# A graph convolution that gathers node rows: two columns of x by one addition, fewer row buffers, sums in one place

## The chip, the cores and the metric

The kernel runs on one core of a Trainium2 chip. The metric is the device time of one execution in microseconds, the median of several runs. A profile of one further execution gives the times of single instructions.

## The reference

There are 12,500 nodes with 128 features each (32 scalars and 32 vectors of three) and 412,500 directed edges, sorted by their destination. For each edge the features of the source node, multiplied by a weight matrix, are combined with weights that a small network makes from the 8 radial inputs of the edge; the messages are summed for each destination, multiplied once more, added to x, and normalised over the features.

```python
f0 = x0 @ W1_0e / sqrt(MUL);  f1 = einsum('nui,uw->nwi', x1, W1_1o) / sqrt(MUL)
feat0, self0 = f0[:, :MUL], f0[:, MUL:];  feat1, self1 = f1[:, :MUL], f1[:, MUL:]
e0 = feat0[edge_src];  e1 = feat1[edge_src]            # one row per edge
h = gelu(gelu(edge_scalar_attr @ W_mlp1 / sqrt(8)) @ W_mlp2 / sqrt(64))
w00, w01, w10, w11 = h @ Wp_00, h @ Wp_01, h @ Wp_10, h @ Wp_11
out0_a = w00 * e0 * ea0;  out0_b = w11 * sum(e1 * ea1[:, None, :], -1) / sqrt(3)
out1_a = (w01 * e0)[:, :, None] * ea1[:, None, :];  out1_b = w10[:, :, None] * e1 * ea0[:, :, None]
n0, n1 = segment_sum(concat(out0_a, out0_b)), segment_sum(concat(out1_a, out1_b))   # by edge_dst
y = cos(MIX) * self + sin(MIX) * (n0 @ W2_0e, n1 @ W2_1o)
return layernorm(x + y)
```

## The kernel before, in words

**Tiling.** The edges are cut into 806 runs of 512 (`NS`), a run into four blocks of 128 (`Q`). Two runs make a pair (`PR`, 403 of them), four a chunk (`CH`, 202). The main loop goes over pairs. The order of the instructions of PE, ACT, DVE and SP is the order of the program, written out by hand; POOL only issues gathers, in their own order, and each waits for its buffer.

**Where a block's rows come from.** Each block of 128 edges needs 128 feature rows in a tile `G` (edge by feature). There are five ways:

- An indirect DMA of POOL gathers 128 rows by index from a table in DRAM (`gather`, L223). The table holds all nodes' features and is made by the preamble (`turn`, `features_of`, `store_nodes`).
- DVE copies single columns out of `xT`, the transposed x that lies in SBUF, at addresses that it loads into registers (`fetch`, L174; `copy_columns`, L188); 128 of these make a tile that PE multiplies by the weights (L197), and ACT writes the product into `G` (L198). This serves block 2 of some runs.
- ACT does the same for block 1 of other runs (L192).
- SP copies the rows of block 3 singly, 128 DMAs of one row, for every 14th run from run 36 (`aid`, L204 and L208).
- The first 18 runs (`RAW`) come before the table is there: POOL gathers rows of x itself, which PE turns and multiplies (`turn_rows`, `features`, L616).

`SLOTS` says how many columns DVE and ACT copy at each of their places in a chunk's two pairs: DVE 60 and 68, ACT 56 each. `FROM` is the pair at which this begins, 6. `LEAD` is the number of runs for which there are `G` buffers, 20, ten pairs in all.

**The rest of a pair.** DVE multiplies the weights `w` (in PSUM) and `G` to the messages `M` in three instructions (`messages`: L651, and twice L655), PE sums them by segments (`segments`, L671), DVE places them in the running sums `acc` (`add`, L711), and for each group of 512 nodes (`GN`) that is complete the sums are multiplied and normalised (`norm`, L756 to L777; two groups at a time, `LNB`). The small steps of the normalisation stand in a list `waiting` and are taken between DVE's copies. When the window of sums moves on by 512 nodes, ACT copies `acc` into a second buffer, and DVE clears the new part in the four next pairs (L425). Indices come for 128 runs at a time (`load_indices`, L468 to L485).

Of the kernel before, what the change touches and what calls it, by code (L numbers as in the profile page):

```python
# [21 lines left out]
P = 128  # L22
# [17 lines left out]
LEAD = 20  # L40
# [17 lines left out]
def gnn_kernel(ctx: ExitStack, tc: tile.TileContext, x, src, dst, ea4, ea8, w1_0, w1_1, wm1, wm2,  # L58
# [31 lines left out]
    x_at, _ = nc.bump_sbuf(4 * N)  # L90
    xT = nc.alloc_sbuf_tensor_at("xT", [P, N], F32, offset=x_at).ap()
    x_bytes = xT.bitcast(U8)
    x_bytes = bass.AP(tensor=x_bytes.tensor, offset=x_bytes.offset - x_at, ap=[[4 * N, P], [1, x_at + 4 * N]])
# [16 lines left out]
    G, GP, GT, Y = {}, {}, {}, {}  # L110
# [12 lines left out]
    assert AID_FROM >= raw_runs and AID_LEAD < LEAD and P % ROWS == 0 and STEPS <= AID  # L123
# [7 lines left out]
    def aid_load():  # L131


        nc.sync.dma_start(aid_at, sub(src, AID_FROM * SB + (Q - 1) * P, [[AID * SB, len(aided)], [1, P]]))
        for e, g in picked.items():
            n, w = len(g) * P, per_chunk[e]
            flat = dr.tile([n], I32, name=f"flat{list(picked).index(e)}")
            cycle = next(c for c in range(1, len(g) + 1)
                         if all(g[i + c] - g[i] == g[c] - g[0] for i in range(len(g) - c)))
            for i in range(min(cycle, len(g))):  # L140
                k = len(g[i::cycle])
                step = g[i + cycle] - g[i] if k > 1 else 1
                nc.sync.dma_start(sub(flat, i * P, [[cycle * P, k], [1, P]]),
                                  sub(src, g[i] * SB + COL_Q[e] * P, [[step * SB, k], [1, P]]))
            for r in range(0, -(-n // w), P):
                k = min(P, -(-n // w) - r)
                full, rest = divmod(min(n - r * w, k * w), w)
                rows = cst.tile([k, w], I32, name=f"pick{len(pick_tiles)}")
                if rest:
                    nc.vector.memset(rows, 0)  # L150
                    nc.sync.dma_start(rows[full:full + 1, :rest], sub(flat, (r + full) * w, [[rest, 1], [1, rest]]))
                if full:
                    nc.sync.dma_start(rows[:full], sub(flat, r * w, [[w, full], [1, w]]))
                pick_tiles.append(rows)
                pick_rows[e, r // P] = rows
# [3 lines left out]
    def addresses():  # L159
        nc.vector.tensor_scalar(aid_at, aid_at, float(4 * P), None, op0=OP.mult)  # L160
        for rows in pick_tiles:
            nc.vector.tensor_scalar(rows, rows, 4.0, float(x_at), op0=OP.mult, op1=OP.add)
# [3 lines left out]
    def fetch(e, n):  # L166

        at = taken[e]
        n = min(n, len(picked[e]) * P - at)
        if n <= 0:  # L170
            return []
        taken[e] += n
        row, c0 = divmod(at, per_chunk[e])
        _, r = nc.values_load_multi_w_load_instructions(  # L174
            pick_rows[e, row // P][row % P:row % P + 1, c0:c0 + n], engines=[e], min_val=x_at,
            max_val=x_at + 4 * (N - 1), skip_runtime_bounds_check_because="addresses of columns")
        return [(at + k, r[k]) for k in range(n)]

    def copy_columns(e, columns):

        for at, r in columns:
            i, j = divmod(at, P)
            if j == 0:
                GT[e, i] = wk.tile([P, P], F32, name=f"gt{list(picked).index(e)}", bufs=3)
            to = GT[e, i][:, j:j + 1]
            col = x_bytes[:, bass.ds(r.with_bounds(guaranteed_mod_val=0, out_of_modulus=4), 4)].bitcast(F32)
            if e == DVE:
                nc.vector.tensor_copy(to, col)  # L188
                if waiting and j % 2:
                    waiting.pop(0)()  # L190
            else:
                nc.scalar.activation(to, col, AF.Copy)  # L192
# [7 lines left out]
    def aid(s, t):  # L200

        i = aided.index(s)
# [4 lines left out]
        for k in range(r1 - r0):  # L207
            nc.sync.dma_start(G[s][r0 + k:r0 + k + 1, Q - 1, :].bitcast(U8),  # L208
                              table_bytes[bass.ds(r[k], P * 4)].rearrange("(a k) -> a k", a=1))

    def gather(s):
        b, c = divmod(s, P)
        if s % PR == 0:
            GP[s // PR] = wk.tile([P, PR, Q, P], F32, name="G", bufs=LEAD // PR)
        G[s] = GP[s // PR][:, s % PR]
# [12 lines left out]
    diag = cst.tile([P, P], I32)  # L228
    nc.gpsimd.iota(diag, pattern=[[1, P]], base=0, channel_multiplier=-1)
    iota = cst.tile([P, P], F32)  # L230
# [23 lines left out]
    def load_nodes(b, rows=x):  # L254
        n0, nn, full, tail, _ = group(b)
        xt = wk.tile([P, XB, P], F32, name="xt", bufs=3)
# [32 lines left out]
    def turn(b):  # L289
# [5 lines left out]
        nc.scalar.activation(xT[:, n0:n0 + nn], PX[b][:, :nn], AF.Copy)  # L295

    def features_of(b):
        n0, nn, full, tail, tiles = group(b)
        pf = W2.pop(b)[:, 1].rearrange("p (q e) -> p q e", q=XB)
        for t, k in tiles:  # L300
            nc.tensor.matmul(pf[:k, t, :], xT[:, n0 + t * P:n0 + t * P + k], wf, start=True, stop=True)
        PF[b] = wk.tile([P, XB, P], F32, name="ft", bufs=3)
# [15 lines left out]
    scratch = wk.tile([P, 4, ACC], F32, name="acc")  # L318
# [102 lines left out]
    def new_sums():  # L421
        A["next"] = wk.tile([P, 4, ACC], F32, name="acc")

    def clear_sums(k):
        nc.vector.memset(A["next"][:, k, ACC - GN:], 0.0)  # L425
# [26 lines left out]
    def rows_tile(part=None):  # L452

        if part is None:
            return wk.tile([P, XB, P], F32, name="xt", bufs=3).rearrange("p q e -> p (q e)")
# [5 lines left out]
    def load_indices(b):  # L461
        ns = min(P, NS - b * P)
        idx[b] = wk.tile([P, Q, P], I32, name="idx")
        rel[b] = wk.tile([P, Q, P], F32, name="rel")
        colv[b] = wk.tile([P, P], F32, name="colv")
        for kind, raw in zip((1, 0), raws.pop(b)):
            f = wk.tile([P, XB, P], F32, name="ft", bufs=3).rearrange("p q e -> p (q e)")
            nc.vector.tensor_copy(f[:ns, :], raw[:ns, :])  # L468
            if kind:
                g = wk.tile([P, XB, P], F32, name="ft", bufs=3).rearrange("p q e -> p (q e)")  # L470
# [53 lines left out]
    def load_attributes(b):  # L524
        full, rest = divmod(min(E - b * P * P, P * P), P)
        t = e4_raw[b] = rows_tile(None if b else 2)
# [7 lines left out]
    def turn_attributes(b):  # L534
# [4 lines left out]
        e4[b] = wk.tile([P, 4, P], F32, name="e4")  # L539
# [63 lines left out]
    def turn_rows(s):  # L603
# [4 lines left out]
        XR[s] = wk.tile([P, Q, P], F32, name="xt", bufs=3)  # L608
# [35 lines left out]
    def messages(p, part):  # L644
        n = min(PR, NS - p * PR)
        if part == 0:
            M[p] = wk.tile([P, PR, Q, 2, P], F32, name="M")
        w, g, m = (t[:, :n].rearrange(f"p r q {k} -> p (r q) {k}") for t, k in
                   ((WP[p], "u"), (GP[p], "u"), (M[p], "a u")))
        if part == 0:  # L650
            nc.vector.tensor_tensor(m[:, :, :, :MUL], w[:, :, :2 * MUL].rearrange("p q (a u) -> p q a u", a=2),  # L651
                                    g[:, :, None, :MUL].to_broadcast([P, n * Q, 2, MUL]), op=OP.mult)
            return
        j = part - 1
        nc.vector.tensor_tensor(m[:, :, j, MUL:].rearrange("p q (i u) -> p q i u", i=3),  # L655
                                w[:, :, None, (2 + j) * MUL:(3 + j) * MUL].to_broadcast([P, n * Q, 3, MUL]),
                                g[:, :, MUL:].rearrange("p q (i u) -> p q i u", i=3), op=OP.mult)

    def segments(p):
# [3 lines left out]
        if r == 0:  # L663
            SEG[c] = ps.tile([P, CH, P], F32, name="seg", bufs=1)
            SG[c] = wk.tile([P, CH, P], F32, name="sg")
# [13 lines left out]
    def placing(c):  # L679
# [3 lines left out]
        PL[c] = wk.tile([P, CH, P], F32, name="pl")  # L683
# [19 lines left out]
    def add(c):  # L703
# [6 lines left out]
        a = A["now"][:, :, bass.ds(FIRST.pop(c), SPAN)]  # L710
# [7 lines left out]
    def moments(b, sums=None, half=None):  # L718
# [14 lines left out]
        for t, k in tiles:  # L733
            nc.tensor.matmul(pt[:k, t - t0, :], xT[:, n0 + t * P:n0 + t * P + k], ws, start=True, stop=sums is not None)
            if sums is None:
                for a in range(4):
                    nc.tensor.matmul(pt[:k, t - t0, :], A["now"][:, a, at + t * P:at + t * P + k], wpost[:, a, :],
# [105 lines left out]
    def general():  # L843
        T = max(t for t in range(1, P + 1) if E % t == 0)
        sums = dr.tile([N + P, P], F32)
        zero = wk.tile([P, XB, P], F32, name="ft", bufs=3)
# [4 lines left out]
        below = cst.tile([P, P], F32)  # L851
        nc.vector.tensor_scalar(below, diag, 0.0, None, op0=OP.is_lt)
# [100 lines left out]
    with tc.manual_schedule(engines={PE, ACT, DVE, SP}):  # L953
# [4 lines left out]
        for s in range(min(LEAD - 2, raw_runs)):  # L958
# [4 lines left out]
        for b in range(min(3, NG)):  # L963
# [4 lines left out]
        new_sums()  # L968
# [3 lines left out]
                 NG // 2 + 1: lambda: nc.vector.memset(A["next"], 0.0),  # L972
                 NG - 3: run_places}
        for b in range(NG + 2):
# [6 lines left out]
            if b + 3 < NG:  # L981
                XT[b + 3] = load_nodes(b + 3)
# [5 lines left out]
        for c in range(1, min(EDGES_AHEAD, NCH)):  # L988
            load_edges(c)
# [4 lines left out]
        for c in range(1, min(3, NCH)):  # L994
            radial(c)
# [11 lines left out]
        A["now"] = A["next"]  # L1007
# [16 lines left out]
        for p in range(NP):  # L1024
            c, k = divmod(p, CH // PR)
            mine = [s for s in range(p * PR, (p + 1) * PR) if s < NS]
            if p:
                for s in mine:
                    if s + LEAD - PR < NS:
# [15 lines left out]
            if k == 0:  # L1045
                placing(c)
                if c + 1 < NCH:
                    hot_rows(c + 1)
# [18 lines left out]
            if k == 0 and c > 0:  # L1067
                place(c - 1)
                placed = c
            if nets:  # L1070
# [6 lines left out]
            for s in mine:  # L1077
                if s % ET == 20 and s - 20 + ET < NS:
# [17 lines left out]
            if moved:  # L1096
                new_sums()
                clearing += list(range(4))
            elif clearing:
                clear_sums(clearing.pop(0))  # L1100
# [5 lines left out]
            picks(DVE, p, 2)  # L1106
            if k == 1 and placed > added:
# [8 lines left out]
            if p == 0:  # L1116
                addresses()
                find_first()
                new_sums()
                clearing = list(range(4))  # L1120
# [10 lines left out]
        for c in range(added, NCH):  # L1131
            if c >= placed:
                place(c)
            if moving and moving[0] + 2 == c:
                move_sums()
                moving.pop(0)
            add(c)
# [37 lines left out]
```

## Time and profile before

| | |
|---|---|
| median of 3 runs | 3540.56 us (3540.39 to 3550.26) |
| the profiled execution's own time | 3552.97 us |
| its span, first to last instruction | 3551.2 us |
| busy: PE, DVE, ACT, POOL | 73%, 88%, 81%, 75% |
| table gathers of POOL (L223) | 2728, mean 945 ns |
| column copies of DVE (L188) | 25,216 |
| column copies of ACT (L192) | 21,888 |
| row DMAs of SP (L208) | 7040 |
| mean granted TensorE clock | 0.819 |

A row of the costliest groups gives line, engine, operation, the tiles out and in, the count, the busy time and the mean duration in ns, and the idle time of the engine just before them with what ended most of it. A row of the timeline gives the start and the duration in us, then the same names. "issue" is time in which the engine waited for nothing that the profile shows.

### The profile page before, as it was taken

What the parts mean: (1) busy time and instruction counts of PE and PEld (TensorE: products, weight loads), DVE (VectorE), ACT (ScalarE), POOL (GpSimd) and SP (SyncE); (2) the same over time, 40 slices, a digit from 0 to 9 for tenths busy, and PEclk for the clock granted to TensorE, in tenths of its full rate; (3) what the DMA queues carried; (4) which work ended last, traced back from release to release, by engine and by line L of the source; (5) the groups of instructions that cost most, each with busy time, mean ns of one, the idle gap of its engine ahead of it and who ended that gap; (6) DMA issues with size and microseconds to landing.
All of it is one profiled execution on the core that took longest, in us unless ns stands there. A gap on an engine that the chain in (4) does not pass through costs nothing.

```text
span 3551.2 us, 141354 instructions
## 1 busy us (share of the span) xinstructions
PE 2577.7 (73%) x30219; PEld 1955.6 (55%) x30219; DVE 3113.3 (88%) x27933; ACT 2884.6 (81%) x24128; POOL 2647.6 (75%) x2807
## 2 busy tenths in 40 slices
PE   6777677777777777777776677676777777677775
PEld 5555555555555555555555555555555555555554
DVE  3499999999999988998988998888898888899886
ACT  2489889888898887888888788888798797788883
POOL 7677777777777777777777777777777777777775
PEclk9888888888788877788777787878788877788778
DMA  8222222223222222222222222222222222222221
GB/s 199 65 57 72 64 60 70 63 61 75 63 64 66 63 61 69 68 61 63 68 60 69 69 61 63 65 64 68 64 63 63 61 69 63 62 68 63 61 65 46
DMA packets 576956, 239.39 MB, mean 67 GB/s; under 512 B 481293, under 2 KB 526456, under 8 KB 576088
## 3 DMA queue, kind: packets, MB, share of 16 engines
q0 software_dynamic: 89600, 183.68, 18.0%
q1 hardware_dynamic: 465718, 40.13, 9.1%
q10 hardware_dynamic: 20770, 6.47, 0.8%
q8 instruction: 244, 4.00, 0.4%
q14 instruction: 624, 5.11, 0.4%
HBM read 217.25 MB, written 12.99 MB: 65 GB/s over the span
## 4 chain that ended last, share of the span: by engine, by line
DVE 35%; POOL 15%; issue 11%; ACT 10%; PE 9%; DMA 6%; SPq 6%; DVEq 4%; ACTq 1%; POOLq 0%
DVE gt L188 19%; POOL G L223 15%; DVE M L655 7%; ACT gt L192 7%; DMA G<-table,idx 6%; SPq L208 4%; DVEq L174 4%; DVE M L651 3%; DVE S L640 2%; PE w L598 2%; SPq L204 1%; PE m L698 1%; DVE pl L684 1%; DVE acc L711 1%; ACT h L560 1%
## 5 line engine op out<-in xcount | busy, mean ns | idle before, releaser
L223 POOL DMA_INDIRECT G<-table,idx x2728 | 2578.4, 945 | 853.3 <-issue 734.3
L192 ACT ACTIVATE gt<-xT 128x1 f32 x21888 | 2192.7, 190 | 116.3 <-issue 94.7
L188 DVE COPY gt<-xT 128x1 f32 x25216 | 1674.6, 144 | 141.4 <-issue 118.3
L655 DVE TENSOR_TENSOR M<-w,G 128x768 f32<-128x768 f32 x806 | 760.7, 944 | 0.0
L671 PE MATMUL seg<-M,S 128*32 128x128 f32 x12896 | 573.0, 323 | 122.1 <-DVE M L655 120.2
L571 PE MATMUL h<-h,w2b 64*64 64x256 f32 x3232 | 399.1, 516 | 311.6 <-ACT eT L546 208.6
L671 PEld LDWEIGHTS seg<-M,S 128*32 128x32 f32 x12896 | 393.3, 128 | 312.9 <-DVE M L655 178.9
L598 PE MATMUL w<-wpb,h 64*128 64x128 f32 x6448 | 565.3, 325 | 0.0
L598 PEld LDWEIGHTS w<-wpb,h 64*128 64x128 f32 x6448 | 476.5, 223 | 61.4 <-issue 27.0
L651 DVE TENSOR_TENSOR M<-w,G 128x512 f32<-128x512 f32 x403 | 275.4, 683 | 171.2 <-DMA G<-table,idx 64.5
L571 PEld LDWEIGHTS h<-h,w2b 64*64 64x64 f32 x3232 | 175.0, 169 | 437.2 <-ACT eT L546 259.6
L560 ACT ACTIVATE h<-h 128x512 f32<-128x512 f32 x404 | 234.9, 582 | 206.7 <-PE h L555 194.1
L197 PE MATMUL h<-wf,gt 128*128 128x128 f32 x736 | 202.0, 378 | 258.3 <-DVE gt L188 136.0
L197 PEld LDWEIGHTS h<-wf,gt 128*128 128x128 f32 x736 | 134.4, 237 | 349.6 <-issue 124.6
L698 PE MATMUL m<-pl,sg 128*128 128x128 f32 x1612 | 282.6, 329 | 20.8 <-ACT sg L677 20.3
L698 PEld LDWEIGHTS m<-pl,sg 128*128 128x128 f32 x1612 | 278.5, 245 | 30.0 <-ACT sg L677 26.2
L555 PE MATMUL h<-eT,w1b 64*128 64x128 f32 x3232 | 279.3, 304 | 21.1 <-ACT eT L546 14.8
L577 ACT ACTIVATE h<-h 128x512 f32<-128x512 f32 x404 | 234.5, 582 | 56.6 <-PE h L571 54.8
L555 PEld LDWEIGHTS h<-eT,w1b 64*128 64x128 f32 x3232 | 233.3, 205 | 57.9 <-ACT eT L546 15.0
L677 ACT ACTIVATE sg<-seg 128x256 f32<-128x256 f32 x403 | 148.7, 369 | 140.4 <-PE seg L671 135.5
L640 DVE TENSOR_TENSOR S<-oh,m 128x512 f32<-128x512 f32 x202 | 134.7, 667 | 9.5 <-ACT m L633 8.5
L684 DVE TENSOR_TENSOR pl<-m,colv 128x512 f32<-128x512 bf16 x202 | 137.1, 679 | 0.0
(123 smaller groups left out, 1491.8 us busy)
## 6 DMA issues: line engine op xcount, KB each, us to landing
G<-table SPq DMA_DIRECT2D x7040, 0.5 KB
G<-table,idx POOLq DMA_INDIRECT x2728
e<-in_edge_attr SPq DMA_DIRECT2D x201, 64.0 KB
xt<-in_x SPq DMA_DIRECT2D x24, 256.0 KB
table<-ft ACTq DMA_DIRECT2D x24, 256.0 KB
xt<-in_edge_attr SPq DMA_DIRECT2D x24, 256.0 KB
out<-y SPq DMA_DIRECT2D x24, 256.0 KB
xt<-in_dst SPq DMA_DIRECT2D x5, 256.0 KB
```

What stands on the lines that cost most here:

```text
L188: nc.vector.tensor_copy(to, col)
L192: nc.scalar.activation(to, col, AF.Copy)
L197: nc.tensor.matmul(pt, GT.pop((e, i)), wf, start=True, stop=True)
L223: nc.gpsimd.indirect_dma_start(out=G[s][:, q, :], out_offset=None, in_=x if s < raw_runs else table, in_offset=bass.IndirectOffsetOnAxis(a ...
L555: nc.tensor.matmul(p1[h][:, j // 2, j % 2, :], w1b[rows, j, :], eT[c][rows, :], start=True, stop=True)
L560: nc.scalar.activation(H1[c][h], P1[c][h].rearrange("p k j e -> p (k j e)"), AF.Gelu_apprx_tanh, scale=1.0 / math.sqrt(RAD))
L571: nc.tensor.matmul(p2[r][k * HID:(k + 1) * HID, h * n:(h + 1) * n], w2b[rows, :], H1[c][h][rows, k * n:(k + 1) * n], start=True, stop=True)
L598: nc.tensor.matmul(WP[p][:, i, q, :], H2[c][q % 2][rows, k, q // 2, :], wpb[rows, :], start=True, stop=True)
L651: nc.vector.tensor_tensor(m[:, :, :, :MUL], w[:, :, :2 * MUL].rearrange("p q (a u) -> p q a u", a=2), g[:, :, None, :MUL].to_broadcast([P, ...
L655: nc.vector.tensor_tensor(m[:, :, j, MUL:].rearrange("p q (i u) -> p q i u", i=3), w[:, :, None, (2 + j) * MUL:(3 + j) * MUL].to_broadcast ...
L671: nc.tensor.matmul(SEG[c][q * W:(q + 1) * W, r + i, :], own[:, (r + i) * Q + q, h * W:(h + 1) * W], M[p][:, i, q, h, :], start=h == 0, sto ...
L698: nc.tensor.matmul(to[:, :, bass.ds(k_at, 4 * W)].bitcast(F32), SG[c][:, k, :], PL[c][:, k, :].rearrange("p (a n) -> p a n", a=4), start=F ...
```

## The change

x is kept in blocks of 512 columns with a gap of 512 zero columns before, between and behind them (`xs`, twice as wide as `xT`). One `tensor_tensor` addition of DVE makes two columns: its first input is a view of two columns 512 apart that begins at the first wanted column, so that the second of the view lies in a gap and is zero; its second input begins 512 columns before the second wanted one, so that its first is zero. The addresses for this are worked out once, in more steps (`addresses`). DVE's slots go to 80 columns, 40 additions, in each pair; ACT's stay; both begin at pair 10.

The space for this comes from elsewhere. `LEAD` goes from 20 to 8 runs. The rows of the 18 raw runs, the x rows and the features of the preamble lie in the gaps, which are set to zero when they have been used: two gaps in each of pairs 0 to 8, eight in pair 9. The messages of raw pairs are multiplied run by run. The sums `acc` are one buffer that is moved in place, all four parts cleared in the following pair; the first clearing of 128x3136 moves from the preamble into pair 0. The normalisation takes one group at a time. SP's rows come into a tile of their own, `GA`, of one buffer, and DVE copies them into `G` ahead of the pair's messages. Several tiles have fewer buffers (`e8` 2 for 4, `e4`, `sg`, `pl` 1, `xt` and `ft` 2 for 3), and indices as numbers are kept in bf16. `placing` goes from the first to the second pair of a chunk.

```diff
-LEAD = 20
+LEAD = 8
-AID_LEAD = 16
+AID_LEAD = 12
-SLOTS = {DVE: ((20, 20, 20), (20, 16, 20, 12)), ACT: ((12, 16, 16, 12), (12, 16, 16, 12))}
-FROM = {DVE: 6, ACT: 6}
+SLOTS = {DVE: ((28,24,28),(24,20,24,12)), ACT: ((12, 16, 16, 12), (12, 16, 16, 12))}
+FROM = {DVE: 10, ACT: 10}
-LNB = 2
+LNB = 1
...
+    XW = 2 * GN * (NG - 1) + GN + (N - (NG - 1) * GN) + GN
+    xs = nc.alloc_sbuf_tensor_at("xs", [P, XW], F32, offset=x_at).ap()
...
+    def x_block(b):
+        return xs[:, (2 * b + 1) * GN:min((2 * b + 2) * GN, XW - GN)]
+    def gap(b):
+        return xs[:, 2 * b * GN:min((2 * b + 1) * GN, XW)]
...
     def addresses():
-        for rows in pick_tiles:
-            nc.vector.tensor_scalar(rows, rows, 4.0, float(x_at), op0=OP.mult, op1=OP.add)
+        for e, rows in pick_tiles:
...
+            nc.vector.tensor_scalar(blocks, rows, GN.bit_length() - 1, None, op0=OP.logical_shift_right)
+            nc.vector.tensor_scalar(rows, rows, 4.0, float(x_at + 4 * GN), op0=OP.mult, op1=OP.add)
+            nc.vector.scalar_tensor_tensor(rows, blocks, float(4 * GN), rows, op0=OP.mult, op1=OP.add)
+            if e == DVE:
+                nc.vector.tensor_scalar(rows[:, 1::2], rows[:, 1::2], -4.0 * GN, None, op0=OP.add)
...
     def copy_columns(e, columns):
-        for at, r in columns:
+        for k in range(0, len(columns), 1 if e == ACT else 2):
+            at, r = columns[k]
...
-            if e == DVE:
-                nc.vector.tensor_copy(to, col)
-                if waiting and j % 2:
-                    waiting.pop(0)()
+            a, b = (words(v, 4 * GN + 4)[:, ::GN] for _, v in columns[k:k + 2])
+            nc.vector.tensor_tensor(GT[e, i][:, j:j + 2], a, b, op=OP.add)
+            if waiting:
+                waiting.pop(0)()
...
     def aid(s, t):
+        if t == 0:
+            GA[s] = wk.tile([P, P], F32, name="ga", bufs=1)
...
-            nc.sync.dma_start(G[s][r0 + k:r0 + k + 1, Q - 1, :].bitcast(U8),
+            nc.sync.dma_start(GA[s][r0 + k:r0 + k + 1, :].bitcast(U8),
...
     def gather(s):
-        if s % PR == 0:
+        if s < raw_runs:
+            G[s] = gap_rows(s)
+        elif s % PR == 0:
             GP[s // PR] = wk.tile([P, PR, Q, P], F32, name="G", bufs=LEAD // PR)
...
     def move_sums():
-        nc.scalar.activation(A["next"][:, :, :ACC - GN], A["now"][:, :, GN:], AF.Copy)
-        A["now"] = A["next"]
+        nc.scalar.activation(acc[:, :, :ACC - GN], acc[:, :, GN:], AF.Copy)
...
-        e8[b] = wk.tile([P, CH, Q, RAD], F32, name="e8", bufs=EDGES_AHEAD)
+        e8[b] = wk.tile([P, CH, Q, RAD], F32, name="e8")
...
+        if p * PR < raw_runs:
+            views = [(WP[p][:, i], G[p * PR + i], M[p][:, i]) for i in range(n)]
...
-        for s in range(min(LEAD - 2, raw_runs), min(LEAD, NS)):
+        for s in range(raw_runs, min(raw_runs + LEAD, NS)):
             gather(s)
...
-                    if s + LEAD - PR < NS:
+                    if s >= raw_runs + PR and s + LEAD - PR < NS:
                         gather(s + LEAD - PR)
...
+            for s in mine:
+                if s in aided:
+                    nc.vector.tensor_copy(G[s][:, Q - 1, :], GA.pop(s))
...
             messages(p, 2)
             picks(DVE, p, 2)
+            if p == raw_runs // PR:
+                for b in range(raw_runs, NG + 1):
+                    nc.vector.memset(gap(b), 0.0)
+            if mine[0] < raw_runs:
+                for s in mine:
+                    nc.vector.memset(gap(s), 0.0)
...
             if p == 0:
                 addresses()
                 find_first()
-                new_sums()
-                clearing = list(range(4))
+                nc.vector.memset(acc, 0.0)
```

More of the change, by code (lines that the diff above doesn't have):

```diff
@@ L316, in gnn_kernel @@
     ones = cst.tile([P, 1], F32)
-    scratch = wk.tile([P, 4, ACC], F32, name="acc")
+    acc = cst.tile([P, 4, ACC], F32)
+    scratch = acc
     def line(i, dtype=F32):
@@ L850, in general @@
         nc.sync.dma_start(sums[N:, :], zero[:, 0, :])
-        below = cst.tile([P, P], F32)
-        nc.vector.tensor_scalar(below, diag, 0.0, None, op0=OP.is_lt)
+        apart, below = differences()
+        nc.vector.tensor_scalar(below, apart, 0.0, None, op0=OP.is_lt)
         spare = cst.tile([P, 1], F32)
@@ L957, in gnn_kernel @@
             load_raw_rows(nc.scalar, 3, raw_runs)
-        for s in range(min(LEAD - 2, raw_runs)):
+        for s in range(raw_runs):
             gather(s)
@@ L1006, in gnn_kernel @@
             features(s)
-        A["now"] = A["next"]
         clearing = []
@@ L1136, in gnn_kernel @@
                 moving.pop(0)
+                for i in range(4):
+                    clear_sums(i, N - base[-1] + SPAN if c == NCH - 1 else ACC)
             add(c)
```

134 lines of the change are left out of this document (72 added, 62 removed).

## The prediction

> **What bounds the kernel now.** I read the page first, then the waits, then POOL's instructions in order of time. The span and the busy shares come first, then the costliest groups and the wait that is charged to POOL's gathers.
>
> ```profile
> span 3551.2 us, 141354 instructions
> PE 2577.7 (73%) x30219; PEld 1955.6 (55%) x30219; DVE 3113.3 (88%) x27933; ACT 2884.6 (81%) x24128; POOL 2647.6 (75%) x2807
> L223 POOL DMA_INDIRECT G<-table,idx x2728 | 2578.4, 945 | 853.3 <-issue 734.3
> L188 DVE COPY gt<-xT 128x1 f32 x25216 | 1674.6, 144 | 141.4 <-issue 118.3
> L655 DVE TENSOR_TENSOR M<-w,G 128x768 f32<-128x768 f32 x806 | 760.7, 944 | 0.0
> L651 DVE TENSOR_TENSOR M<-w,G 128x512 f32<-128x512 f32 x403 | 275.4, 683 | 171.2 <-DMA G<-table,idx 64.5
> POOL G L223 <- issue: 755.9, 2477, 0.8
> ```
>
> DVE has the highest busy share, and the change takes work from DVE. But DVE is not the limit of the run as a whole. POOL issues 2800 gathers (2728 from the table and 72 raw ones); its idle time is almost all "issue", 755.9/2477 = 0.305 us each, which no producer ends. So a gather costs 0.945 + 0.305 = 1.25 us, and 2800 of them make 3500 us of the 3551. The next view is POOL alone, at the places where it did wait, and at its last gather.
>
> ```profile
> 92.47 0.94 POOL L223 DMA_INDIRECT G<-in_x,idx_raw  x1 [0.30 <-issue]
> 105.96 0.95 POOL L223 DMA_INDIRECT G<-table,idx  x1 [12.55 <-DMA table<-ft]
> ...
> 120.98 0.94 POOL L223 DMA_INDIRECT G<-table,idx  x1 [5.33 <-ACT h L560]
> ...
> 196.20 0.94 POOL L223 DMA_INDIRECT G<-table,idx  x1 [3.82 <-ACT h L560]
> ...
> 3524.15 0.95 POOL L223 DMA_INDIRECT G<-table,idx  x1 [0.31 <-issue]
> ```
>
> From 105.96 to 3524.15, 2727 intervals lie in 3418.19 us: 2727 x 1.25 = 3408.8, and the two waits shown (5.33 and 3.82, less the ordinary 0.3 each) make 8.6 of the remaining 9.4. So after the table is there, POOL's queue is the path, with 3551.2 - 3525.1 = 26.1 us of tail behind its last gather. What the change is worth is read from POOL: how many gathers it removes, and what new waits it puts into that queue.
>
> **DVE's part: worth nothing in itself.** Before, DVE copies 25,216 columns one at a time; after, 15,552 additions take 31,104 columns.
>
> ```profile
> 1800.75 1.30 DVE L188 COPY gt<-xT 128x1 f32 x20
> L174 DVEq TENSOR_LOAD <-pick x1379: 845/1358/2271, 163.6 to 3508.3; - x197
> ```
>
> A copy's pace is 1.30/20 = 65 ns, 1639 us in all; at the same pace the additions take 1011 us. By this DVE gives up 628 us, but of POOL's queue none of it. [...]
>
> An addition may be dearer than a copy, with two register addresses and a step of 2 KB. DVE's other work is (3113.3 - 1674.6)/403 = 3.57 us a pair of runs. POOL will want a pair every 8.49 us (2651 gathers for 390 pairs, below), so DVE becomes the limit only above (8.49 - 3.57)/40 = 0.123 us an addition. The register loads grow from 20 to up to 28 columns: at 1358 ns for the usual 20 that is some 0.5 us longer for each of 1361. They run ahead of the engine, as the 118.3 us of "issue" before all copies shows; I cost them at nothing, since DVE has over 2 us of slack a pair; without that cover they would cost up to 0.5 x 3.4 = 1.7 us a pair.
>
> **Fewer gathers.** 64 columns a pair become 80 on DVE, so DVE picks 243 blocks instead of 197, ACT 170 instead of 171 (starting at pair 10 instead of 6). The instruction order gives 2683 table gathers instead of 2728: 45 x 1.25 = **-56.2 us**, all on the path.
>
> **The start: a new wait.** Before, ten pairs of G buffers let POOL run ahead. After, there are four, and the 18 raw runs lie in the gaps. POOL gathers the raw runs, waits for the table until 105.96 as before, gathers runs 18 to 25 (32 gathers, to 105.96 + 32 x 1.25 = 146.0), and then needs the buffer of pair 9, which is free when DVE has done pair 9's messages. When is that? The first pairs are paced by turning and multiplying the raw rows:
>
> ```profile
> 117.80 0.69 DVE L651 TENSOR_TENSOR M<-w,G 128x512 f32<-128x512 f32 x1 [4.73 <-ACT G L616]
> 120.27 0.60 DVE L162 TENSOR_SCALAR pick<-pick 128x128 int32<-128x128 int32 x4
> 123.93 0.69 DVE L651 TENSOR_TENSOR M<-w,G 128x512 f32<-128x512 f32 x1 [0.85 <-ACT G L616]
> 126.48 0.94 DVE L655 TENSOR_TENSOR M<-w,G 128x768 f32<-128x768 f32 x1
> 130.73 1.08 PE L671 MATMUL seg<-M,S 128*32 128x128 f32 x32
> 131.47 0.69 DVE L651 TENSOR_TENSOR M<-w,G 128x512 f32<-128x512 f32 x1 [3.25 <-ACT G L616]
> 163.54 0.69 DVE L651 TENSOR_TENSOR M<-w,G 128x512 f32<-128x512 f32 x1 [3.27 <-ACT G L616]
> 196.79 0.69 DVE L651 TENSOR_TENSOR M<-w,G 128x512 f32<-128x512 f32 x1
> 318.66 0.69 DVE L651 TENSOR_TENSOR M<-w,G 128x512 f32<-128x512 f32 x1
> 62.21 2.67 DVE L972 MEMSET acc<- 128x3136 f32 x1 [0.60 <-DVE ft L304]
> L425 DVE MEMSET acc<- 128x512 f32 x96 | 46.6, 485 | 5.3
> ```
>
> Between pairs 0 and 1 DVE now also clears the sums (2.67, moved here from the preamble), clears two gaps (2 x 0.485) and works out longer addresses (about 11 more steps at 0.60/4, 1.7 us): 5.3 us, and with split messages and their small steps I take 6.3. Pair 1's messages move from 123.93 to 130.2 and end 3.5 us later (126.48 + 0.94 - 123.93) at 133.7. PE's segments of pair 1 stood at 130.73, so only 133.7 - 130.73 = 3.0 is passed on to the turning of later rows. Pair 6 comes at 163.54 + 3 = 166.5. Before, picking starts at pair 6 and pairs 6 to 9 take 33.3 us. After, it starts at pair 10, so pairs 7 and 8 keep the pace of 131.47 to 163.54 (four pairs, 8.0 each): 182.5. Pair 9 isn't raw; DVE needs 4.3 from pair 8's messages to its own (messages 2.4, two gap clears 1.0, the rest small steps): 186.8, and its messages end near 190. The gap clears of pairs 1 to 8 lie in DVE's wait for G (3.25 and 3.27 above) and cost nothing; without that cover they would be 1 us a pair.
>
> POOL thus idles 190 - 146 = 44 us, where it idled 8.6: **+35.5 us**. Ends: 186 (no delay handed on) to 200 (pairs 7 and 8 stretched as before), +31 to +45. The last gather ends at 3525.1 - 56.2 + 35.5 = 3504.
>
> **Later waits.** Four buffered pairs cover 4 x 8.49 = 34 us of DVE's lateness, where ten covered 86. DVE's own pace while it catches up shows between pair 9 (196.79) and pair 25 (318.66): 121.87/16 = 7.6 us a pair, with copies. That is under 8.49, and additions make it shorter, so after the restart POOL stays the later one; I add nothing, 0 to 5. Normalising one group at a time (LNB 1) doubles the small steps and puts a dozen behind the last gather, the aid copies add 55 x 0.3 on DVE; together **+3** (0 to 6).
>
> **POOL's reads against additions.** Here an unseen cost can come in: the additions take two SBUF inputs, where a copy takes one and the messages take one (w comes from PSUM). The timeline beside a short operation with two SBUF inputs (L775), a one-input CAST, and two long ones with two inputs (L447) shows this:
>
> ```profile
> 324.83 0.15 DVE L775 SCALAR_TENSOR_TENSOR rs<-rs 128x4 f32<-128x4 f32 x1
> 324.91 0.94 POOL L223 DMA_INDIRECT G<-table,idx  x1 [0.30 <-issue]
> 377.39 0.42 DVE L468 CAST ft<-xt 128x512 f32<-128x512 int32 x1
> 377.40 1.22 POOL L223 DMA_INDIRECT G<-table,idx  x1 [0.31 <-issue]
> 378.78 0.69 DVE L447 TENSOR_TENSOR ft<-ft,off 128x512 f32<-128x512 f32 x1
> 378.92 1.36 POOL L223 DMA_INDIRECT G<-table,idx  x1 [0.30 <-DVE off L446]
> 899.31 0.94 POOL L223 DMA_INDIRECT G<-table,idx  x1 [0.30 <-DVE off L442]
> 899.86 0.69 DVE L447 TENSOR_TENSOR ft<-ft,off 128x512 f32<-128x512 f32 x1
> ```
>
> A gather that begins inside L447's 0.69 us takes 1.36 instead of 0.94, +0.42; one that begins inside the short L775 takes 0.94, and so does one that is 0.55 us old when the other L447 begins. So a gather seems to be held where it meets such an operation early, until that ends. The additions are running 15,552 x 0.065/3400 = 0.30 of the time. If each hit holds the gather for half an addition, 0.30 x 0.033 x 2651 = +26 us; if it waits out a whole unbroken run of 14 additions (0.91 us, half on average), 0.30 x 0.455 x 2651 = +362. If short ones never hold it, 0. I take **+5**, near the row of the short operation, which is the nearest in length, and keep 0 to +26.
>
> [...]
>
> **Sum.** -56.2 + 35.5 + 3 + 5 = -12.7 on the profiled execution, whose own time is 3552.97 for the span of 3551.2. The median of the runs shown is 3540.56, 12 below the profiled one; the same difference on it gives **3528 us**. A measurement of this kernel can tell about 0.3% (10.6 us) from no change, so this stands at the edge of "faster".
>
> **Rivals.**
>
> *Reads held by additions (slower, if anything).* With +26 the sum is +8: 3549. The rows speak for it at 0.69 us and against it at 0.15. With whole runs held, 3885.
>
> *The aid loop with one buffer (slower).* SP's 128 row loads for one block now go into one tile GA that DVE must empty before SP starts on the next.
>
> ```profile
> 710.13 18.57 SPq L208 DMA_DIRECT2D G<-table  x48
> 730.64 18.62 SPq L208 DMA_DIRECT2D G<-table  x48
> 751.21 11.66 SPq L208 DMA_DIRECT2D G<-table  x32
> 3516.65 2.45 DMA G<-table,idx
> ```
>
> The issues take 762.87 - 710.13 = 52.7 us, landing some 2.45 more (by a gather's), the copy 0.3: 55.5 us, every 14 runs, in which POOL takes 7 x 8.49 = 59.4. There are 3.9 us to spare. An edge load ahead of a row load on SP now waits for one of two e8 buffers instead of four; if that holds SP over 3.9 us in each round, SP decides. At 61 us a round: 55 x 1.6 = +88, 3616.
>
> *DVE after all (slower).* Above 0.123 us an addition: at 0.15 it is 40 x 0.027 x 393 = +424. The 65 ns row speaks against it.
>
> *A shorter start (faster).* If pair 9 is done at 186, no gather is held and the tail is as before: -56.2 + 31 = -25, 3515.
>
> *It does not pay at all.* The saved gathers only move the wait: if the stretched start (+45), tail and reads (+11) eat 56, 3540.
>
> **Chances.** Forecast 0.46: 0.34 over 10.6 us faster, since the short row would make the +5 a 0, and 0.12 within. Shorter start 0.11, faster. Reads held at +26 0.12: +8 alone is within (0.04), with the upper ends of start and tail it is slower (0.08). Nothing gained 0.04, within. Aid loop 0.18, since its spare is only 3.9 of 59.4 us. DVE or whole runs held 0.09. Faster 0.45, within 0.20, slower 0.35. The range runs from 3507 (8 below the shorter start, for the small terms that were rounded up) to 3575 (reads held with both upper ends, or a mild aid loop); it leaves out the larger aid loop, DVE and whole runs.
>
> **What would show it.** Right: 2683 table gathers 1.25 us apart, POOL idle about 44 us before the 33rd of them, restart near 190, last gather ending near 3504, additions near 65 ns. Wrong: a mean gather above 950 ns or "issue" above 0.31 (reads held); DVE waiting at the GA copy for DMA (aid loop); POOL's waits after 200 us ended by DVE's messages (DVE or too few buffers).

## The result, and the profile after

The changed kernel takes 3747.78 us (median of 4 runs, 3735.99 to 3759.05), the kernel before 3544.39 (4 runs, 3540.39 to 3550.26): a ratio of 1.0572, 95% interval 1.0533 to 1.0612. The prediction said 3528, at most 3575. The profiled execution of the changed kernel took 3735.99, 183.0 more than the 3552.97 of the kernel before.

One condition is needed to read the experiments: in fourteen of the eighteen runs below, the kernel before, run beside them, itself took 5910 to 5990 us, at a granted clock of 0.67 to 0.69 (0.82 in the profile of before), so that their times say little of this change, and only those of e8, e14, e15 and e16, where it took 3547 to 3552, are read as times of it.

The page of the changed kernel, its span, busy shares and costliest groups; then the lines of its waits that carry the argument (total, times, longest):

```profile
span 3734.2 us, 131757 instructions
PE 2622.2 (70%) x30309; PEld 1961.9 (53%) x30309; DVE 2794.3 (75%) x18554; ACT 2907.3 (78%) x24047; POOL 2608.6 (70%) x2762
L248 POOL DMA_INDIRECT G<-table,idx x2683 | 2539.6, 947 | 1069.5 <-issue 866.9
L210 DVE TENSOR_TENSOR gt<-xs 128x2 f32 x15552 | 1288.6, 155 | 612.4 <-issue 594.6
...
POOL G L248 <- issue: 866.9, 2441, 7.7
DVE gt L210 <- issue: 594.6, 989, 2.1
...
POOL G L248 <- DVE M L686: 79.0, 26, 44.9
```

DVE's busy time fell from 3113.3 to 2794.3, but the wait that ends in "issue" before its picks rose from 118.3 to 594.6. POOL, which never waited over 0.8 us for "issue" before, now waits up to 7.7. POOL in order of time shows where:

```profile
93.52 0.94 POOL L248 DMA_INDIRECT G<-table,idx  x1 [0.30 <-issue]
...
132.80 0.94 POOL L248 DMA_INDIRECT G<-table,idx  x1 [0.30 <-issue]
178.62 0.94 POOL L248 DMA_INDIRECT G<-table,idx  x1 [44.88 <-DVE M L686]
...
2253.98 0.94 POOL L248 DMA_INDIRECT G<-table,idx  x1 [0.31 <-issue]
2261.06 0.94 POOL L248 DMA_INDIRECT G<-table,idx  x1 [6.13 <-issue]
...
3701.37 0.94 POOL L248 DMA_INDIRECT G<-table,idx  x1 [0.30 <-issue]
```

The wait of 44.88 is the forecast start gap. After it POOL should be 2650 x 1.25 = 3312 us from its last gather; it took 3522.8. Between 250 us and the end there are 81 waits over 0.4 us like the one at 2261.06, together 206.6 us beyond the ordinary 0.3. That closes the account of the 183.0: the last gather starts 3701.37 - 3524.15 = 177.2 later; fewer gathers (-56.2), the table that was ready earlier (-12.4) and the longer waits at the start (+35.5) give -33.1, the waits after 250 us +206.6, and gathers that lie a little further apart the remaining +3.7; and the tail behind the last gather grew from 26.1 to 31.9, +5.8.

What POOL waits for is a free row buffer, and so DVE, though the profile puts most of these waits down to "issue". In the program the first gather of a pair needs the buffer that is free once DVE has made the last messages of the pair four before. Of the 81 gathers, 65 start 0.76 us and 10 start 0.27 us after the end of such a last message instruction, and 0.27 is also the delay after the wait of 44.88, which the profile puts down to DVE's `M`. The one at 2261.06 follows this one, which ends at 2260.30:

```profile
2259.35 0.95 DVE L686 TENSOR_TENSOR M<-w,G 128x768 f32<-128x768 f32 x1
```

A steady pair of DVE in the changed kernel, from the first of its 28-column slots on, then the register loads as the trace counts them, all together and the two of this stretch:

```profile
2238.07 0.67 DVE L682 TENSOR_TENSOR M<-w,G 128x512 f32<-128x512 f32 x1
2240.02 1.14 DVE L210 TENSOR_TENSOR gt<-xs 128x2 f32 x14 [1.27 <-issue]
2241.08 0.94 DVE L686 TENSOR_TENSOR M<-w,G 128x768 f32<-128x768 f32 x1
2242.25 0.97 DVE L210 TENSOR_TENSOR gt<-xs 128x2 f32 x12 [0.23 <-issue]
...
L191 DVEq TENSOR_LOAD <-pick x1361: 842/1640/2628, 177.9 to 3691.2; - x195
L191 DVEq TENSOR_LOAD <-pick x1: 1891/1891/1891, 2238.0 to 2238.0; - x1
L191 DVEq TENSOR_LOAD <-pick x1: 1641/1641/1641, 2240.5 to 2240.5; - x1
```

Each group of additions first needs its addresses in registers. By size, the median load in the two kernels takes 867, 1125, 1382, 1640 and 1897 ns for 12, 16, 20, 24 and 28 columns; the prediction's 1358 was the median over loads of 12, 16 and 20. While these two ran, DVE had only what was queued ahead of them: 0.67 us of messages cover part of the load of 28 columns that begins at 2238.0, and 1.27 us are left; the end of the additions and 0.94 us of messages cover most of the load of 24 that begins at 2240.5, and 0.23 are left. Before, a group of 20 copies ran 1.30 us and its load 1.38, so most of the loads were covered: the waits for "issue" before the copies were 118.3 us in all. Over the stretch from 250 to 3450 us (columns: PE, its weight loads, DVE, ACT, POOL, clock, DMA share, GB/s), after and then before:

```profile
250.00:3450.00 3200.00, 2257.76 (x26189) 1678.25 (x26186) 2448.55 (x16629) 2589.90 (x21792) 2277.88 (x2408) 0.79 0.26 61
```

```profile
250.00:3450.00 3200.00, 2345.00 (x27755) 1766.91 (x27757) 2910.73 (x26542) 2719.82 (x23120) 2419.49 (x2560) 0.81 0.28 65
```

And DVE's waits of the changed kernel in that stretch:

```profile
DVE gt L210 <- issue: 540.6, 902, 2.1
DVE pl L715 <- ACT m L659: 100.2, 50, 6.2
DVE G L1079 <- DMA ga<-table: 60.4, 13, 9.5
```

After, DVE is busy 2448.6 and waits in this stretch 540.6 for loads, 100.2 for ACT's `m` and 60.4 for SP's rows: 3149.8 of 3200. For want of gathered rows it is idle 1.4 us in this stretch (`M L682 <- DMA G<-table,idx`, 6 times). DVE had become the limit, with a share of busy time that looks lower than before. Over all pairs, the median time by which the first gather of a pair comes after the earliest that its buffer allows is 1.8 us.

### The profile page after: what moved, and what is told of

The parts are those of the page before. It is cut to its first block, busy times and chain, and to the rows that moved or that the text cites. A ratio compares the mean times of both kernels' runs of the same rounds, so it can differ in the third digit from the quotient of the medians.

```text
span 3734.2 us, 131757 instructions
## 1 busy us (share of the span) xinstructions
PE 2622.2 (70%) x30309; PEld 1961.9 (53%) x30309; DVE 2794.3 (75%) x18554; ACT 2907.3 (78%) x24047; POOL 2608.6 (70%) x2762
## 5 line engine op out<-in xcount | busy, mean ns | idle before, releaser
L248 POOL DMA_INDIRECT G<-table,idx x2683 | 2539.6, 947 | 1069.5 <-issue 866.9
L207 ACT ACTIVATE gt<-xs 128x1 f32 x21760 | 2181.3, 190 | 177.0 <-issue 154.5
L210 DVE TENSOR_TENSOR gt<-xs 128x2 f32 x15552 | 1288.6, 155 | 612.4 <-issue 594.6
L702 PE MATMUL seg<-M,S 128*32 128x128 f32 x12896 | 597.8, 322 | 527.2 <-DVE M L686 524.3
L624 PE MATMUL w<-wpb,h 64*128 64x128 f32 x6448 | 630.1, 352 | 0.0
L624 PEld LDWEIGHTS w<-wpb,h 64*128 64x128 f32 x6448 | 536.4, 248 | 73.9 <-issue 49.8
L597 PE MATMUL h<-h,w2b 64*64 64x256 f32 x3232 | 374.5, 539 | 149.2 <-ACT eT L572 100.1
L217 PE MATMUL h<-wf,gt 128*128 128x128 f32 x826 | 232.3, 392 | 118.0 <-DVE gt L210 39.4
L729 PEld LDWEIGHTS m<-pl,sg 128*128 128x128 f32 x1612 | 251.9, 226 | 44.7 <-ACT sg L708 21.5
L682 DVE TENSOR_TENSOR M<-w,G 128x512 f32<-128x512 f32 x394 | 268.4, 681 | 7.2 <-DMA G<-table,idx 1.4
L570 PE MATMUL h<-ident,e 128*128 128x128 f32 x202 | 75.3, 373 | 102.1 <-ACT G L218 78.6
```

The lines of the kernel that those rows point to most:

```text
L207: nc.scalar.activation(GT[e, i][:, j:j + 1], words(r, 4), AF.Copy)
L210: nc.vector.tensor_tensor(GT[e, i][:, j:j + 2], a, b, op=OP.add)
L217: nc.tensor.matmul(pt, GT.pop((e, i)), wf, start=True, stop=True)
L248: nc.gpsimd.indirect_dma_start(out=G[s][:, q, :], out_offset=None, in_=x if s < raw_runs else table, in_offset=bass.IndirectOffsetOnAxis(a ...
L597: nc.tensor.matmul(p2[r][k * HID:(k + 1) * HID, h * n:(h + 1) * n], w2b[rows, :], H1[c][h][rows, k * n:(k + 1) * n], start=True, stop=True)
L624: nc.tensor.matmul(WP[p][:, i, q, :], H2[c][q % 2][rows, k, q // 2, :], wpb[rows, :], start=True, stop=True)
```

## The experiments

Four theories stand against each other. A: the register loads make DVE the limit. B: four pairs of row buffers, one sums buffer and one group at a time make it late. C: the additions themselves are dear. D: the rows that SP copies come late, through their single buffer or otherwise.

**Fixed addresses (e1, e5, e8).** DVE loads no registers; the additions are as many and of the same form.

```diff
+        if e == DVE:
+            return [(at + k, None) for k in range(n)]
...
-            a, b = (words(v, 4 * GN + 4)[:, ::GN] for _, v in columns[k:k + 2])
+            a, b = (xs[:, c:c + GN + 1:GN] for c in (GN + at % GN, (at + 1) % GN))
```

> The changed kernel, but the 15,552 additions take fixed columns instead of addresses in registers, so DVE loads no registers; everything else stands (the picked columns are therefore other ones). Theory A (register loads): in the changed kernel DVE is the limit of every pair, because its additions wait 594.6 us in all for their 28-column loads; POOL's stalls only follow. Then the stalls go: POOL restarts at about 179 and 2651 gathers of 1.25 us and a tail of 33 us end at about 3525 to 3560. Theory B (room): four row buffers, one sums buffer and one group at a time make DVE late at each normalisation whatever the loads do: 3690 or more. Theory C (dear additions, 73 to 83 ns each): the additions are the same here, so 3690 or more as well.

> The first experiment again, on a chip on which the kernel before takes about 3540 us: the changed kernel with its 15,552 additions at fixed columns, so that DVE loads no registers (the picked columns are other ones). Theory A (DVE is the limit through its register loads, 594.6 us of waiting): 3525 to 3560, since POOL restarts at 179 and 2651 gathers of 1.25 us and a tail of 33 us follow. Theory B (four row buffers, one sums buffer, one group at a time) or C (the additions themselves): 3690 or more.

> The changed kernel with its 15,552 additions at fixed columns, so that DVE loads no registers (the picked columns are other ones), a third time, for a chip on which the kernel before takes about 3540 us. Theory A (register loads make DVE the limit): 3525 to 3560. Theory B (row buffers, one sums buffer, one group at a time) or C (the additions themselves): 3690 or more.

e8: 3627.44 against 3550.29 for the kernel before, ratio 1.0218 (1.0188 to 1.0247). So without the loads 77 us remain of some 200: C falls as the main cause, since all additions are still there, and the loads (A) are about 120 us. But theory A alone had said 3525 to 3560, so it is not the whole; B's and C's 3690 or more failed too. In e8's waits:

```profile
DVE pl L717 <- ACT m L661: 592.7, 183, 10.9
...
DVE G L1081 <- DMA ga<-table: 176.9, 40, 13.3
```

The line of loads is gone, POOL's waits after 250 us are 110.5 instead of 206.6, and DVE now waits for other things. e1 and e5 gave 5903.58 and 5897.90, ratios 0.9981 (0.9958 to 1.0005) and 0.9958 (0.9940 to 0.9977). DVE waits 626.4 and 659.5 us for "issue" before its additions there, though it loads nothing. But only 8.1 and 6.9 us of this lie before the first addition of a group, which is where a load is waited for; so that place can be compared between the runs.

**Size and place of the loads (e2, e7, e10, e18; e4, e6, e11).** With the slots of the kernel before, and with the same 160 columns in more places, first at any offset, then at multiples of four:

```diff
-SLOTS = {DVE: ((28,24,28),(24,20,24,12)), ...
+SLOTS = {DVE: ((20, 20, 20), (20, 16, 20, 12)), ...                 # e2, e7, e10, e18
+SLOTS = {DVE: ((14, 22, 24), (14, 12, 22, 16, 22, 14)), ...         # e4
+SLOTS = {DVE: ((16, 20, 24), (16, 12, 20, 16, 20, 16)), ...         # e6, e11
```

> The changed kernel with DVE's slots of the kernel before, 60 and 68 columns a pair, so loads of at most 20 columns; 2731 gathers from the table and 195 picked blocks on DVE instead of 2683 and 243. Theory A: the waits for loads fall from 594.6 us to 120 to 200, DVE has room again and POOL sets the end: 179 + 2699 x 1.25 + 33 = 3585, up to 3620 with some stalls. Theory B: the normalisations stay as late, and the time stays at 3700 to 3770.

> The changed kernel with DVE's slots of the kernel before, 60 and 68 columns a pair: additions with register addresses, loads of at most 20 columns, 2803 gathers from the table instead of 2683; SP's rows as in the changed kernel (one buffer, AID_LEAD 12). Loads: their waits fall from 594.6 us to 90 to 200. POOL's work is 177 + 2771 x 1.25 less the 40 us before... that is 177 + 2699 x 1.25 + 30 = 3581. If POOL's slower pace (8.65 us a pair instead of 8.49) is what removes the stalls, 3580 to 3605. If the late rows of SP cost stalls of their own, 100 us as with fixed columns: 3650 to 3690. If the loads were not the main cause: 3740 or more.

> The changed kernel with the same 160 columns a chunk, but in nine places instead of seven: (14, 22, 24) and (14, 12, 22, 16, 22, 14), each load behind one longer DVE operation. Theory A: a load of 22 is covered by 0.95 us of messages and the additions still queued, so the waits for loads fall from 594.6 us to about 300, DVE falls below POOL, and the time is 3540 to 3620. Theory B or C: 3700 or more, as the work and the buffers are the same.

> The changed kernel with its 160 columns a chunk in nine places, all counts and so all load offsets multiples of four: (16, 20, 24) and (16, 12, 20, 16, 20, 16). The run of e4 waited 4.0 us for loads of 22 columns that began at column 14 or 86, and 0.73 for one that began at column 124; if that is the offset, DVE's waits for loads are here below those of the changed kernel (594.6 us), about 250 to 350. Theory A: then 3540 to 3640. Theory B or C: 3700 or more. If the loads don't like the places and not the offsets: above 3750.

e7 and e10 repeat e2 and e18, and e11 repeats e6, with other expected times. (e18's text counts the 72 raw gathers in its 2803; from the table there are 2731.) The times of the small slots are those of the kernel before (e2 1.0019, 0.9990 to 1.0048; e7 1.0021, 1.0000 to 1.0043; e10 0.9942, 0.9922 to 0.9962; e18 0.9999, 0.9973 to 1.0026), which confirms nothing. Their waits do tell something. DVE's waits before the first addition of a group, added up over a run, are 7 to 11 us without loads (e1, e5, e9, e13, e17), 562 with the changed kernel's slots (e3; 589 in the changed kernel itself), and 290 to 298 with loads of at most 20. So the smaller loads cost half, but not the 90 to 200 that was expected of them. The kernel before, with loads of the same sizes and two copies where these have one addition, waits 112. That fits half the instructions being half the cover, though its trace is from a run of 3553 us and theirs are from runs of over 5900. Spreading the loads over more places did not help: 596 (e6) and 587 (e11) where e6's text had 250 to 350, and these runs took 1.0424 (1.0391 to 1.0458) and 1.0378 (1.0342 to 1.0415) of the kernel before. Theory A's expectation for the spread failed there, and why it cost time is open. e4 stands out:

```profile
L210 DVE TENSOR_TENSOR gt<-xs 128x2 f32 x15552 | 1311.7, 156 | 3028.4 <-issue 3018.6
```

```profile
L210 DVE TENSOR_TENSOR gt<-xs 128x2 f32 x15552 | 1377.0, 156 | 1037.5 <-issue 1029.7
```

The first row is e4, the second e6, with the same number of loads at the same places. In e4, four of the nine loads of a chunk begin at column 14, 74, 86 or 146, no multiple of four, and it waits 2.9 times as long (ratio of times 1.0985, 1.0943 to 1.1026). The loads themselves show it; here are two of 22 columns in e4, from column 14 and from column 124:

```profile
L191 DVEq TENSOR_LOAD <-pick x1: 5083/5083/5083, 2820.3 to 2820.3; - x1
L191 DVEq TENSOR_LOAD <-pick x1: 1869/1869/1869, 2844.0 to 2844.0; - x1
```

**The buffer of SP's rows (e3, e14).**

```diff
-            GA[s] = wk.tile([P, P], F32, name="ga", bufs=1)
+            GA[s] = wk.tile([P, P], F32, name="ga", bufs=2)
```

> The changed kernel with two buffers for SP's row tile GA instead of one. If the single buffer decides (the aid loop of the prediction), the time falls by 150 us or more. Theory A: DVE is the limit and loses only its own wait at the copy, 72 us in 15 places, so 3680 to 3715. Theory B: at most 30 us of it is seen, 3715 to 3745.

> Additions at fixed columns (no register loads on DVE, other columns picked) and two buffers for SP's row tile GA. Fixed columns alone gave 3627, with 110.7 us of POOL stalls after the start; 33 us of these follow within two pairs on a wait for the rows in GA, the others on normalisations and index loads. If the single buffer is the rest: 3530 to 3570. If the four row buffers are: only those 33 go, 3585 to 3605.

e3 (with register loads) gave 5925.43, ratio 1.0019 (0.9998 to 1.0040), nothing to read. e14, with fixed addresses, gave 3627.94, as e8 did; the wait at the copy stayed:

```profile
DVE G L1081 <- DMA ga<-table: 166.7, 38, 13.4
```

So the single buffer, my rival for the slower side, is not the cause. The same trace shows what makes the rows late. SP, then DVE:

```profile
1157.88 0.41 SPq L540 DMA_DIRECT2D e<-in_edge_attr  x1
1178.85 0.41 SPq L296 DMA_DIRECT2D out<-y  x1
...
1229.38 5.13 SPq L232 DMA_DIRECT2D ga<-table  x16
...
1235.87 0.23 DVE L1081 COPY G<-ga 128x128 f32<-128x128 f32 x1 [11.87 <-DMA ga<-table]
```

SP stood from 1158 to 1179 behind the store of a normalised group, and the last 16 rows of the block left at 1229 to 1235, with DVE already waiting. The other late blocks are like it. SP issues a block's rows in some 53 us and takes the next block 2 us later, so what it loses at a store it makes up only over the next blocks. Of the 55 blocks, 45 had a store that held SP over 2 us during their issue, just ahead of it, or in the block before; they have 163 of the 167 us, the other ten 4. (Repeats of this kernel, e9 and e13, had 5964.65, ratio 0.9972, and 5882.33, ratio 0.9945; e12, the aligned spread with two buffers, 6223.05, ratio 1.0394.)

**No rows by SP, with four and five pairs of row buffers (e15, e16).** Both with fixed addresses; the 55 blocks come by POOL's gathers. They also leave out the tables of DVE's addresses and have two buffers instead of three for the tiles of picked columns. The two differ in LEAD alone.

```diff
-    aided = range(AID_FROM, NS - 1, AID)
+    aided = range(0)
...
 LEAD = 8      # e15, as in the changed kernel
+LEAD = 10     # e16
```

> The control of the next run: the changed kernel with additions at fixed columns (no register loads on DVE, other columns picked), no rows by SP (the 55 blocks come by gathers, so 2738), two buffers instead of three for the tiles of picked columns, four pairs of row buffers. POOL's work is 177 + 2706 x 1.25 + 28 = 3588. Theory B (room): with the stalls that follow normalisations and index loads, some 70 us, 3650 to 3670.

> The same with five pairs of row buffers. Theory B: DVE was at most 33 us behind POOL in the runs with fixed columns and POOL stalled from about 20 on; one more pair moves this to 28.5, so most of the stalls go and the time is 3590 to 3620, at least 30 below the control. If DVE's average rate is the limit and not the room, the same as the control within 10.

e15: 3587.11 (3580.74 to 3593.48), ratio 1.0109 (1.0044 to 1.0174). e16: 3575.45 (3570.06 to 3579.08), ratio 1.0082 (1.0058 to 1.0105). Theory B's number for e15, 3650 to 3670, failed: it comes out at POOL's bare work of 3588. e15's waits and its last gather:

```profile
POOL G L248 <- issue: 777.6, 2549, 0.7
DVE pl L715 <- ACT m L659: 521.2, 185, 9.1
...
DVE M L682 <- DMA G<-table,idx: 197.0, 113, 5.0
...
3562.70 0.95 POOL L248 DMA_INDIRECT G<-table,idx  x1 [0.30 <-issue]
```

After 250 us POOL has not one wait over 0.4, with four pairs; the first gather of a pair never comes less than 4.0 us after the earliest that its buffer allows, and the median is 17.1 (4.8 in e8). DVE waits for POOL's rows again, 113 times, as in the kernel before. The 521.2 us that DVE waits for ACT's `m` are thus slack in this run; whether the 592.7 of e8 are is not shown. So four pairs, one sums buffer and one group at a time are room enough here. With five pairs the start gap is 30.3 instead of 42.7 (POOL restarts at 174.63 against 177.38 with eight more gathers done), which is as much as the 12 us between the medians.

**Rows issued earlier (e17).** Two buffers and AID_LEAD 16, fixed addresses.

> Additions at fixed columns (no register loads on DVE, other columns picked), two buffers for GA, and AID_LEAD 16 as in the kernel before instead of 12: SP begins a block's row copies 16 runs ahead and ends 6 ahead, where the changed kernel ends 2 ahead. With two buffers alone DVE still waited 167 us for the rows and 3628 was measured; without the rows by SP POOL did not stall at all after the start. If the rows come late because they are issued late, these waits and the 102 us of stalls go: 3520 to 3540. If only the slower pace of POOL without the rows by SP removed the stalls: 3595 to 3630.

5892.72, ratio 0.9955 (0.9929 to 0.9982), so its question of time stays open. But the wait at the copy of GA, 38.1 and 51.9 us in e9 and e13 with the same two buffers and AID_LEAD 12, doesn't appear in e17 at all. So issued earlier, the rows are in time. The kernel before, with AID_LEAD 16, had 6.6 us of such waits (its `M` for rows by SP):

```profile
DVE M L651 <- DMA G<-table: 6.6, 6, 1.8
```

Where the kernel before took some 3550 us, no version beat it: even with fixed addresses the new layout stays 28 us (e16, without SP's rows) to 77 us (e8) behind it. The ratios just under 1 elsewhere, down to 0.9942, are too small to be read as gains.

## Why the prediction was wrong

**What held.** POOL sets the pace where DVE is in time: e15's last gather starts at 3562.7, and 177.4 + 2705 x 1.25 is 3558.7. 2683 table gathers came, so -56.2 was right. The start gap was forecast at 44 us and is 44.88; it lies 11 us earlier than forecast (restart 178.62, not 190), since the preamble ended earlier: the table was ready at 93.5 and not at 105.96, and DVE's first messages came at 103.3 and not at 117.8. Both ends of the gap moved alike, so that its length came out to the microsecond is in part luck. That the loads of x run four deep there may be why the preamble is shorter; no run tested it.

**The step that failed** is in the part on DVE, worth nothing in itself: the register loads "run ahead of the engine ... I cost them at nothing, since DVE has over 2 us of slack a pair; without that cover they would cost up to 0.5 x 3.4 = 1.7 us a pair". The cover was not there: DVE's waits for the loads are 594.6/403 = 1.48 us a pair, 1.18 of it new, of the size of the bound that I wrote down and left out. e8 shows what this costs, 120 of the 203 us. The cover before was largely the copies themselves, 1.30 us for a load of 20 columns that takes 1.38; the change shortened the cover (14 additions, 1.14) and lengthened the load (28 columns, 1.90). The slack was also too large: it left out all waits and took an addition at 65 ns. With 1288.6/15,552 = 83 ns, 40 additions are 3.3 us a pair, the rest of the busy time 3.74 and the loads 1.48: 8.5 against POOL's 8.49, before any other wait. The rival "DVE after all" was the right one, but I gave its threshold of 0.123 us to the additions alone; with its share of the waits for loads (594.6/15,552 = 38 ns) an addition took 0.121.

**"Later waits", 0 to 5,** rested on this: "additions make it shorter" than 7.6 us a pair. Six pairs of the changed kernel:

```profile
1888.23 0.69 DVE L682 TENSOR_TENSOR M<-w,G 128x512 f32<-128x512 f32 x1
...
1937.23 0.68 DVE L682 TENSOR_TENSOR M<-w,G 128x512 f32<-128x512 f32 x1
```

49.0/6 = 8.2 us, in a quiet stretch. That leaves 0.3 us a pair to POOL's 8.49, too little to win back soon what a normalisation or an index load sets DVE back. Of the 206.6 us that POOL waits, where I had at most 5, 145.9 fall within 20 us after the statistics of a normalisation or the conversion of new indices on DVE, stretches that make up 18% of the time.

**The rows by SP** I priced by their buffer (3.9 us to spare), and did not price AID_LEAD from 16 to 12 at all. Of the 110.5 us that POOL waits without the loads, none are left without these rows. That removal also slowed POOL by 55 gathers, 0.17 us a pair, while it gave DVE back 176.9/403 = 0.44 a pair. In e8, 38.8 of the 110.5 us come within 20 us after a wait of over 1 us at the copy, and 70.1 within 20 us after a normalisation or an index load; both are gone in e15. How much of this is due to the rows and how much to POOL's pace was to be told by e17 and is open.

**Small terms.** The tail grew by 5.8 where I had +3 for it and the aid copies, at most 6. The additions hold gathers hardly at all: the 997 gathers that begin while one runs take 948.8 ns on average, the other 1686 945.2, which is 3.6 us in all; in e8, with as many additions, it is 944.4 against 945.1. So the +5 was of the right size, and 0 would have been as good. Nothing near the rival's +26 shows. My row at 377.40, where a gather beside a one-input cast took 1.22 us, should have warned me that a longer gather need not have two inputs beside it.

## What to carry to other kernels

Here additions with register addresses cost DVE the loads of these registers too, 594.6 us of waits in the profiled run. How much of a load was hidden went with the work queued just ahead of it: 118.3 us of waits were left where groups of 20 copies ran 1.30 us and their loads 1.38, and 594.6 where groups of 14 additions ran 1.14 and their loads 1.90. Fewer instructions are also less cover: for 20 columns 10 additions ran 0.80 us in e14. Look at the engine's busy time and its "issue" together: DVE went from 88% to 75% busy and became the limit. And before fewer buffers are called enough, compare the average pace of the consumer, with its periodic extra work, to that of the producer: where they are 0.3 us a pair apart, a wait of 10 us needs more than thirty pairs to heal.

## What the runs showed of the hardware

A DVE load of addresses into registers took 867, 1125, 1382, 1640 and 1897 ns for 12, 16, 20, 24 and 28 columns (medians in the kernels before and after), 64 ns more for each further column, and the additions that waited for it began 90 ns after its end.

Where a load began made a difference: in e4, 22 columns took 5.08 us from column 14 or 86 and 1.87 from column 124; 12 columns took 2.81 us from column 74, and 0.87 from column 76 in e6. So did the count: 14 columns from column 0 took 1.35 us in e4, 16 took 1.13 in e6. All the beginnings in e4 that are no multiple of four leave 2; others were not run.

Additions with two strided SBUF inputs took 83 ns each in busy time and began 73 to 75 ns apart within a group, where copies of one column began 61 ns apart. The gathers that POOL began beside them took 949 ns on average, the others 945, while one that began inside the 0.69 us of L447 in the kernel before took 1.36 us.
